# Two additions of a graph attention layer issued on GpSimd, with a new pace for the side work

## The chip, the cores and the metric

The kernel runs on one core of a Trainium2 chip. The core has a matrix engine (TensorE, "PE" in the profile, its weight loads "PEld"), a vector engine (VectorE, "DVE"), a scalar engine (ScalarE, "ACT") and a general engine (GpSimd, "POOL"), each with its own instruction queue that runs in order. A fifth queue ("SP") issues most DMAs. Engines meet at semaphores. The metric is the time of one execution on the device, in microseconds, as the median of several runs.

## The reference

Four graph layers run one after another on a graph of N = 2708 nodes with 128 features. Every layer normalises x, applies a ReLU, computes something with the adjacency matrix and adds the result to x. The adjacency is sparse: an entry is not zero with a probability of 0.0015, or on the diagonal, so that a node has some five neighbours, itself among them; the values lie between 0.05 and 1, and the kernel's lists hold up to 16 of them. The layer that matters here is the second:

```python
q = (x @ Wq.T).reshape(d, n, h)      # d = 128 channels, n = 2708 nodes, h = 8
k = (x @ Wk.T).reshape(d, n, h)
v = (x @ Wv.T).reshape(d, n, h)
a = jnp.einsum('dnh,dmh->dnm', q, k) * scale
a = a + spatial_encoding + edge_encoding     # adj + adj
a = jax.nn.softmax(a, axis=2)
out = jnp.einsum('dnm,dmh->dnh', a, v)
out = out.reshape(n, h * d)
return out @ Wo.T
```

So there are 128 attentions ("channels" below) over all 2708 nodes, with a head of 8 values.

## The kernel before

The kernel never forms the 2708 x 2708 attention matrices. The exponential of the small product q.k is written as a polynomial, so that the sum over all m becomes a product of features of q with moments of features of k and v. Where the adjacency is not zero, a correction is added: the weight exp(q.k) times (exp(2 adj) - 1), times v and times one. A column of ones beside the eight columns of v gives the softmax's denominator, so that each result has VW = 9 values, of which the ninth is the share of the denominator.

The polynomial runs in a loop over the 128 channels (variable d), and for each channel over six chunks of up to four node tiles (variable c). There are NT = 22 tiles of 128 nodes, the last with 20. All engines' instructions of this loop are written out in a fixed order by hand (a manual schedule). In each chunk:

- `evaluate` (line 1078 and after) multiplies the transposed features of q (fT) by the weighted moments (mw) on TensorE into g_ps, of which there are two buffers. VectorE multiplies by features bq (z, line 1094) and sums (o_raw, line 1100).
- `queries` makes the next channel's features fq on VectorE (helper line 1007); `turn` transposes them on TensorE, and ScalarE copies them to fT (line 1076).
- `keys` (in the first chunk) makes the features bk and fk of the keys two channels ahead on GpSimd, twelve instructions of helper line 1010; `with_values` makes y in two halves (in the third and the last chunk), one instruction of line 1010 each, into two buffers in turn.
- `moments` multiplies y and fk of the next channel on TensorE into m_ps (line 1048), and `weighted` (line 1058, once a channel) turns the sum into mw on VectorE.
- After every fourth channel (a group; there are 32) `sums` adds the constant term on GpSimd (line 693) and stores the group in o_g.

Beside the loop run two streams of side work, written as generators. The first is the variable `first`. After every chunk `owed` grows by PACE, and while it is at least one, `first` is advanced to its next `yield`; such an advance is called a step here. The stream has, in this order: a search for the neighbours in ten tiles of adjacency (`search`), taking turns with the copies of q, k and v by node (`by_node`); a sort of the nodes by number of neighbours (`in_order`); and the neighbours' terms (`from_neighbours`). The sort lets tile t have only ROOM[t] neighbours, 121 over all tiles. For each of these 121 (index b) `from_neighbours` does:

- `load(b + 1)`: an indirect DMA on GpSimd's queue gathers the k and v of one neighbour for each node (c_kv, line 825, three buffers); at a tile's first neighbour also q (c_q, line 817).
- `logits(b)`: the product q k (c_z, line 840) and its sum over the head (c_c, line 844), both on VectorE, one step each.
- `store()`: where a tile is finished, an indirect DMA on GpSimd's queue writes c_acc to more_n (line 887).
- `values(b - 1)`: v times the weight on VectorE (line 870), the weight itself into the ninth column by ScalarE (line 869), and then the addition to the tile's sum c_acc (line 878). A tile's first neighbour writes c_acc itself, and nothing is added. c_acc has one buffer, so the next tile's first neighbour waits until the store has read it.
- `weigh(b)`: the exponential and the factor from the adjacency on ScalarE.

When `first` is done, the second stream starts, at most three advances a chunk (`step`). It takes entries of the list `beside`, at most two at a time. `normalise(g)` loads a group's sums (ro from o_g, co from more_n, on SP), adds them (line 930), takes the reciprocal of the ninth column (line 932), multiplies (line 933) and stores to o_c. `project_out(t)` loads o_c for a tile, multiplies by Wo on TensorE and adds to x (line 508). An entry may start when its group is below d // 4 - 1. What is left at the end of the loop over channels is done after it.

Layers three and four follow; the change touches nothing in them.

Of the kernel before, what the change touches and what calls it, by code (L numbers as in the profile page):

```python
# [11 lines left out]
ALU = mybir.AluOpType  # L12
# [31 lines left out]
def _cuts(n, w):  # L44

    return [(s, min(w, n - s)) for s in range(0, n, w)]
# [3 lines left out]
def gnn4_kernel(  # L50
# [22 lines left out]
    nc = tc.nc  # L73
# [156 lines left out]
    with ExitStack() as ph:  # L230
# [42 lines left out]
        with tc.manual_schedule():  # L273
# [8 lines left out]
            for t0, tw in _cuts(NT, 4):  # L282
# [3 lines left out]
                for t in range(t0, t0 + tw):  # L286
                    sz = rows[t][1]
# [109 lines left out]
    def to_heads(eng, dst, src, d, t0, nt, n=P):  # L397
        for p0, p1, c, r in runs(d, t0, n):
            eng.dma_start(dst[c : c + p1 - p0, r : r + nt], src[p0:p1])
# [116 lines left out]
    with ExitStack() as ph:  # L516
# [285 lines left out]
        def from_neighbours():  # L802

            nc.scalar.activation(cw, s_val, AF.Exp, scale=2.0)
            yield
            yield
            nc.vector.tensor_scalar_add(cw, cw, -1.0)
            todo = [(t, s0, w) for t in range(NT) for s0, w in _cuts(ROOM[t], S)]
            qs, kvs, cs, accs = {}, {}, {}, {}
            done = []  # L810

            def load(b):
                t, s0, w = todo[b]
                r0, sz = rows[t]
                if s0 == 0:
                    qs[t] = tm.tile([P, C, HEAD], FP, name="c_q", tag="c_q")
                    nc.gpsimd.indirect_dma_start(
                        out=qs[t][:sz].rearrange("p c k -> p (c k)"),
                        out_offset=None,
                        in_=q_n.rearrange("n c k -> n (c k)"),  # L820
                        in_offset=bass.IndirectOffsetOnAxis(ap=s_row[:sz, t], axis=0),
                    )
                kvs[b] = big.tile([P, S, C, 2, HEAD], FP, name="c_kv", tag="big")
                for e in range(w):
                    nc.gpsimd.indirect_dma_start(  # L825
                        out=kvs[b][:sz, e].rearrange("p c e k -> p (c e k)"),
                        out_offset=None,
                        in_=kv_n.rearrange("n c k -> n (c k)"),
                        in_offset=bass.IndirectOffsetOnAxis(
                            ap=s_nbr[:sz, t, s0 + e : s0 + e + 1], axis=0  # L830
                        ),
                    )

            def logits(b):
                t, s0, w = todo[b]
                sz = rows[t][1]
                cs[b] = sm.tile([P, S, C], FP, name="c_c")
                for e in range(w):
                    z = tm.tile([P, C, HEAD], FP, name="c_z", tag="tmp")
                    nc.vector.tensor_tensor(  # L840
                        z[:sz], kvs[b][:sz, e, :, 0], qs[t][:sz], ALU.mult
                    )
                    yield
                    nc.vector.reduce_sum(cs[b][:sz, e], z[:sz], axis=AX.X)
                    yield

            def weigh(b):

                t, s0, w = todo[b]
                sz = rows[t][1]  # L850
                c = cs[b]
                nc.scalar.activation(c[:sz, :w], c[:sz, :w], AF.Exp)
                for e in range(w):
                    nc.scalar.activation(
                        c[:sz, e], c[:sz, e], AF.Copy, scale=cw[:sz, t, s0 + e : s0 + e + 1]
                    )

            def values(b):
                t, s0, w = todo[b]
                sz = rows[t][1]  # L860
                c, kv = cs.pop(b), kvs.pop(b)
                if s0 == 0:
                    accs[t] = lp.tile([P, C, VW], FP, name="c_acc", tag="n_kv")
                acc = accs[t]
                for e in range(w):
                    z = acc
                    if s0 + e:
                        z = tm.tile([P, C, VW], FP, name="c_v", tag="tmp")
                    nc.scalar.copy(z[:sz, :, HEAD], c[:sz, e])
                    nc.vector.tensor_tensor(  # L870
                        z[:sz, :, :HEAD],
                        kv[:sz, e, :, 1],
                        c[:sz, e, :, None].to_broadcast([sz, C, HEAD]),
                        ALU.mult,
                    )
                    yield
                    if s0 + e:
                        nc.vector.tensor_tensor(acc[:sz], acc[:sz], z[:sz], ALU.add)  # L878
                        yield
                if s0 + w == ROOM[t]:  # L880
                    done.append(t)

            def store():
                while done:
                    t = done.pop()
                    sz = rows[t][1]
                    nc.gpsimd.indirect_dma_start(
                        out=more_n.rearrange("n c k -> n (c k)"),
                        out_offset=bass.IndirectOffsetOnAxis(ap=s_row[:sz, t], axis=0),
                        in_=accs.pop(t)[:sz].rearrange("p c k -> p (c k)"),  # L890
                        in_offset=None,
                    )

            load(0)
            if REM:
                none = tm.tile([P, C * VW], FP, name="none", tag="tmp")
                nc.gpsimd.memset(none, 0.0)
                nc.sync.dma_start(
                    more_n[N:].rearrange("n c k -> n (c k)"), none[: NT * P - N]
                )  # L900
            yield
            for b in range(len(todo) + 1):
                if b + 1 < len(todo):
                    load(b + 1)
                    yield
                if b < len(todo):
                    yield from logits(b)
                store()
                if b:
                    yield from values(b - 1)  # L910
                if b < len(todo):
                    weigh(b)
            store()
            yield
            yield

        def normalise(g):

            ro = tm.tile([P, NT, GRP, VW], FP, name="r_raw", tag="tmp")
            co = tm.tile([P, NT, GRP, VW], FP, name="r_more", tag="c_q")  # L920
            nc.sync.dma_start(ro.rearrange("p t i k -> p (t i k)"), o_g[g])
            nc.sync.dma_start(
                co.rearrange("p t i k -> p t (i k)"),
                more_n[:, g * GRP : (g + 1) * GRP].rearrange("(t p) i k -> p t (i k)", p=P),
            )
            for _ in range(AHEAD):
                yield "loaded"
            rs = sm.tile([P, NT, GRP], FP, name="r_rs")
            on = lp.tile([P, GRP, NT, HEAD], FP, name="r_on")
            nc.vector.tensor_tensor(ro, ro, co, ALU.add)  # L930
            yield
            nc.vector.reciprocal(rs, ro[:, :, :, HEAD])
            nc.vector.tensor_tensor(
                on.rearrange("p i t k -> p t i k"),
                ro[:, :, :, :HEAD],
                rs[:, :, :, None].to_broadcast([P, NT, GRP, HEAD]),
                ALU.mult,
            )
            for t0, nt, sz in ((0, NF, P), (NF, 1, REM)):
                for i in range(GRP if sz else 0):  # L940
                    to_heads(nc.sync, o_c, on[:sz, i, t0 : t0 + nt], g * GRP + i, t0, nt, sz)
            yield
# [20 lines left out]
        for t, (r0, sz) in enumerate(rows):  # L963
            need = min((((r0 + sz) * P - 1) // N) // GRP, NG - 1)
            while done <= need:
                beside.append((normalise(done), done, True))
                done += 1
                while late and late[0][1] <= done - 3:
                    beside.append(late.pop(0))
            late.append((project_out(tm, ps_t, woT, t), need, False))  # L970
# [24 lines left out]

        mid = NT // 2
        parts = [(0, mid), (mid, NT)]
        PACE = 1.30
        TM = max(b - a for a, b in parts)
        W = weights()  # L1000
        bks = [lp.tile([P, NT, B_W], FP, name=f"bk{i}") for i in range(2)]
# [104 lines left out]
        with tc.manual_schedule():  # L1106
# [19 lines left out]
            for d in range(D):  # L1126
                asked = queries(d + 1) if d + 1 < D else iter(())
                for c in range(NCH):
# [20 lines left out]
                    n += 1  # L1149
                    owed += PACE  # L1150
                    while owed >= 1 and first is not None:
# [228 lines left out]
    with ExitStack() as ph:  # L1380
# [9 lines left out]
        with tc.tile_pool(name="l3w", bufs=1) as wk_pool, tc.tile_pool(  # L1390
# [21 lines left out]
            z = tp.tile([1, 2 * C], FP, name="tab_z")  # L1412
# [29 lines left out]
        with tc.tile_pool(name="l3_more", bufs=2) as mp, tc.tile_pool(  # L1442
# [28 lines left out]
            with tc.For_i(0, rounds):  # L1471
                for t, (r0, sz) in enumerate(rows):
# [35 lines left out]
                    z = gated(mp, bn[:, t], sz, idx, val, 8)  # L1508
# [34 lines left out]
        for t, (_, sz) in enumerate(rows):  # L1543
# [6 lines left out]
            z = gated(gp, own[:, :C], sz, s_nbr[:, t], s_val[:, t, :k], k)  # L1550
# [51 lines left out]
```

## Time and profile before

| what | us |
|---|---|
| median of 3 runs | 4518.02 (4509.77 to 4524.34) |
| the profiled execution | 4486.52 |
| its span | 4484.7 |
| VectorE busy in the span | 3669.4 |
| GpSimd busy in the span | 2544.8 |
| line 878's additions, 99 of them, mean 2.507 us | 248.2 |
| line 930's additions, 32 of them, mean 1.377 us | 44.1 |

The profile is of one execution. "Busy" counts the time in which an engine has an instruction in work, which may include time in which the instruction itself stands still. A group of instructions is written as line, engine, operation, output<-inputs, partitions x elements, count, then the busy time and the mean duration in ns; what follows the second bar is the idle time of that engine right before these instructions and what ended it. In the row of slices each digit is the busy share, in tenths, of one fortieth of the span (112 us). A line of the order of time gives the start, the duration, the engine, the line and what was done; instructions of the same kind that follow each other are drawn together with their count. A line of waits gives who waited for whom, the total in us, the number of waits and the longest.

### The profile page before, as it was taken

Reading aid. Unit: us, or ns where it says so; the run is one execution under the profiler, and the core shown is the slowest. Engines: PE = TensorE matmul, PEld = TensorE weight load, DVE = VectorE, ACT = ScalarE, POOL = GpSimd, SP = SyncE. Lnnn points to the kernel's source line nnn. Section 1 sums busy time; section 2 is a strip of 40 time slices with the busy share of each in tenths; the row PEclk is TensorE's granted clock in tenths of the full one; section 3 lists DMA queues with packets and bytes.
Section 4 is the critical chain, followed back from the end, with each engine's and each line's share of the span. In section 5 each row is a group of like instructions: output and inputs, shape, how many; then the busy total and the mean of one; then the engine's idle time right before and its main releaser. Section 6 shows DMA issues by size and latency. Waiting matters only on the chain. (4 is left out here: it accounts for less than half of the span.)

```text
span 4484.7 us, 49573 instructions
## 1 busy us (share of the span) xinstructions
PE 3225.3 (72%) x17298; PEld 2876.7 (64%) x17298; DVE 3669.4 (82%) x4983; ACT 1100.2 (25%) x2497; POOL 2544.8 (57%) x2253
## 2 busy tenths in 40 slices
PE   7985778889966677677777676667676687839634
PEld 5952777788856666667666676667666677824323
DVE  5988889998868999999999998999899888831323
ACT  4255233334412222222222222222122111101201
POOL 0001766678858666677676676767576555300076
PEclk9987888999988888888888888888888788959555
DMA  4647334357702222222222222222222344447132
GB/s 186 227 154 294 86 101 110 87 126 171 164 9 84 79 75 76 89 81 83 87 76 88 77 92 78 85 86 94 86 88 88 76 97 95 107 108 262 51 100 79
DMA packets 402005, 480.24 MB, mean 107 GB/s; under 512 B 290672, under 2 KB 322098, under 8 KB 376916
## 3 DMA queue, kind: packets, MB, share of 16 engines
q1 hardware_dynamic: 370140, 308.03, 23.8%
q0 software_dynamic: 31600, 168.86, 11.2%
q8 instruction: 144, 2.36, 0.2%
q14 instruction: 121, 0.99, 0.1%
HBM read 363.13 MB, written 113.67 MB: 106 GB/s over the span
## 5 line engine op out<-in xcount | busy, mean ns | idle before, releaser
L1086 PE MATMUL g_ps<-mw,fT 128*128 128x189 f32 x5632 | 1213.3, 362 | 734.6 <-DVE mw L1058 501.9
L1086 PEld LDWEIGHTS g_ps<-mw,fT 128*128 128x128 f32 x5632 | 1032.8, 213 | 812.8 <-issue 642.2
L1010 POOL TENSOR_TENSOR y<-bk,raw 128x2079 f32<-128x2079 f32 x256 | 982.9, 3840 | 685.7 <-PE m_ps L1048 658.4
L1048 PE MATMUL m_ps<-y,fk 128*128 128x189 f32 (+1 forms) x5632 | 1108.1, 342 | 29.0 <-POOL y L1010 29.0
L1048 PEld LDWEIGHTS m_ps<-y,fk 128*128 128x128 f32 (+1 forms) x5632 | 969.2, 204 | 58.1 <-POOL y L1010 29.5
L1076 ACT COPY fT<-f_ps 128x512 f32<-128x512 f32 (+1 forms) x768 | 422.9, 551 | 1955.2 <-PE f_ps L1074 1954.3
L1094 DVE TENSOR_TENSOR z<-g_ps,bq 128x756 f32<-128x756 f32 (+1 forms) x768 | 669.1, 871 | 177.7 <-PE g_ps L1086 173.9
L1100 DVE TENSOR_REDUCE o_raw<-z 128x36 f32<-128x756 f32 (+1 forms) x768 | 672.5, 876 | 26.3
L1010 POOL TENSOR_TENSOR fk<-bk,raw 128x528 f32<-128x528 f32 (+1 forms) x512 | 526.5, 1058 | 0.0
L1074 PE MATMUL f_ps<-ident,fq 128*128 128x128 f32 x2816 | 490.8, 299 | 46.2 <-DVE fq L1007 44.6
L1074 PEld LDWEIGHTS f_ps<-ident,fq 128*128 128x128 f32 x2816 | 399.2, 157 | 83.9 <-issue 45.8
L1010 POOL TENSOR_TENSOR fk<-raw,bk 128x352 f32<-128x352 f32 (+1 forms) x512 | 337.3, 688 | 0.0
L840 DVE TENSOR_TENSOR c_z<-c_kv,c_q 128x1024 f32<-128x1024 f32 (+1 forms) x121 | 308.1, 2546 | 5.3 <-DMA c_kv<-kv_n,srt 5.3
L1007 DVE TENSOR_TENSOR fq<-bq,q_ps 128x528 f32<-128x528 f32 (+1 forms) x512 | 288.1, 605 | 0.0
L825 POOL DMA_INDIRECT c_kv<-kv_n,srt x121 | 139.1, 1150 | 244.3 <-DVE c_v L870 142.4
L1010 POOL TENSOR_TENSOR bk<-raw 128x88 f32<-128x88 f32 (+1 forms) x512 | 238.3, 496 | 34.6 <-DMA raw<-qkv_c 34.1
L878 DVE TENSOR_TENSOR c_acc<-c_acc,c_v 128x1152 f32<-128x1152 f32 (+1 forms) x99 | 248.2, 2507 | 2.5
L465 POOL MEMSET qkv<- 128x512 f32 x6 | 6.3, 1076 | 373.7 <-PE l_o L350 254.3
L870 DVE TENSOR_TENSOR c_v<-c_kv,c_c 128x1024 f32<-128x1024 f32 (+1 forms) x99 | 205.9, 2080 | 0.0
L1420 POOL DMA_INDIRECT g<-gate_d,srt x121 | 122.0, 1008 | 107.9 <-issue 105.1
L505 PE MATMUL l_o<-woT,o_cr 128*128 128x128 f32 (+1 forms) x352 | 94.8, 425 | 107.6 <-DMA o_cr<-o_c 68.6
L1007 DVE TENSOR_TENSOR fq<-q_ps,bq 128x352 f32<-128x352 f32 (+1 forms) x512 | 171.7, 378 | 0.0
(284 smaller groups left out, 3490.2 us busy)
## 6 DMA issues: line engine op xcount, KB each, us to landing
a_nat<-in_adj_dram SPq DMA_DIRECT2D x32, 1354.0 KB
qkv_c<-qkv SPq DMA_DIRECT2D x5, 6400.0 KB
a<-in_adj_dram SPq DMA_DIRECT2D x21, 1354.0 KB
kv_n<-n_kv SPq DMA_DIRECT2D x32, 672.0 KB
an<-in_adj_dram SPq DMA_DIRECT2D x15, 1354.0 KB
o_g<-o_raw SPq DMA_DIRECT2D x32, 396.0 KB
r_raw<-o_g SPq DMA_DIRECT2D x32, 396.0 KB
r_more<-more_n SPq DMA_DIRECT2D x32, 396.0 KB
```

What stands on the lines that cost most here:

```text
L825: nc.gpsimd.indirect_dma_start(out=kvs[b][:sz, e].rearrange("p c e k -> p (c e k)"), out_offset=None, in_=kv_n.rearrange("n c k -> n (c k) ...
L840: nc.vector.tensor_tensor(z[:sz], kvs[b][:sz, e, :, 0], qs[t][:sz], ALU.mult)
L870: nc.vector.tensor_tensor(z[:sz, :, :HEAD], kv[:sz, e, :, 1], c[:sz, e, :, None].to_broadcast([sz, C, HEAD]), ALU.mult,)
L878: nc.vector.tensor_tensor(acc[:sz], acc[:sz], z[:sz], ALU.add)
L1007: nc.vector.tensor_tensor(o, x, y, ALU.mult)
L1010: nc.gpsimd.tensor_tensor(o, x, y, ALU.mult)
L1048: nc.tensor.matmul(pms[d][:, : B_ALL * VW], fks[d][:sz, t], ys[d, h][:sz, m].rearrange("p k b -> p (k b)"), start=t == 0, stop=t == NT - 1,)
L1074: nc.tensor.transpose(pt[:, m], fqs[d][:, t0 + m], ident)
L1076: nc.scalar.copy(fts[d, c][:, :n], pt[:, :n])
L1086: nc.tensor.matmul(pg[:, m, : B_ALL * VW], ft[:, m], mws[d].rearrange("p k b -> p (k b)"), start=True, stop=True,)
L1094: nc.vector.tensor_tensor(z[:, :n], pg[:, :n, : B_ALL * VW].rearrange("p t (k b) -> p t k b", k=VW), bqs[d % 2][:, t0 : t0 + n, None, :B_A ...
L1100: nc.vector.reduce_sum(ros[g][:, t0 : t0 + n, i], z[:, :n], axis=AX.X,)
```

## The change

Line 878's addition is issued on GpSimd instead of VectorE. A tile's sum c_acc is still first written by VectorE and ScalarE, and then added to by GpSimd. The `yield` that stood behind the addition now stands ahead of it: two steps lie between the product c_v and its addition, and the addition falls into the step that also issues `weigh(b)` and `load(b + 2)`. The second `yield` is outside the condition, so that a tile's first neighbour takes a step more than before. Line 930's addition in `normalise` goes to GpSimd as well, and the reciprocal on VectorE follows it as before. PACE goes from 1.30 to 1.45 steps a chunk.

```diff
@@ -874,9 +874,9 @@
                         ALU.mult,
                     )
                     yield
+                    yield
                     if s0 + e:
-                        nc.vector.tensor_tensor(acc[:sz], acc[:sz], z[:sz], ALU.add)
-                        yield
+                        nc.gpsimd.tensor_tensor(acc[:sz], acc[:sz], z[:sz], ALU.add)
                 if s0 + w == ROOM[t]:
                     done.append(t)
 
@@ -927,7 +927,7 @@
                 yield "loaded"
             rs = sm.tile([P, NT, GRP], FP, name="r_rs")
             on = lp.tile([P, GRP, NT, HEAD], FP, name="r_on")
-            nc.vector.tensor_tensor(ro, ro, co, ALU.add)
+            nc.gpsimd.tensor_tensor(ro, ro, co, ALU.add)
             yield
             nc.vector.reciprocal(rs, ro[:, :, :, HEAD])
             nc.vector.tensor_tensor(
@@ -995,7 +995,7 @@
 
         mid = NT // 2
         parts = [(0, mid), (mid, NT)]
-        PACE = 1.30
+        PACE = 1.45
         TM = max(b - a for a, b in parts)
```

## The prediction

> **What bounds the kernel now.** I began with the page's first two parts: how busy each engine is, and when.
>
> ```profile
> PE 3225.3 (72%) x17298; PEld 2876.7 (64%) x17298; DVE 3669.4 (82%) x4983; ACT 1100.2 (25%) x2497; POOL 2544.8 (57%) x2253
> DVE  5988889998868999999999998999899888831323
> POOL 0001766678858666677676676767576555300076
> ```
>
> VectorE stands at 9 from slice 13 to 30, with GpSimd at 6 or 7. Next, the sums by stretch, cut where the work beside the loop over channels changes: by-node copies, sorting, the neighbours' terms, normalising, and what is left after the loop.
>
> ```profile
> 945.00:1226.00 281.00, 263.03 (x1657) 248.35 (x1658) 240.21 (x406) 117.10 (x228) 229.85 (x214) 0.99 0.73 165
> 1226.00:1372.00 146.00, 91.43 (x505) 85.79 (x505) 92.55 (x147) 24.71 (x56) 100.05 (x117) 0.81 0.10 25
> 1372.00:3528.00 2156.00, 1520.50 (x8281) 1424.84 (x8279) 2047.64 (x2444) 484.14 (x1222) 1487.42 (x1223) 0.84 0.25 83
> 3528.00:3932.00 404.00, 322.68 (x1741) 305.46 (x1741) 327.72 (x491) 64.46 (x147) 202.95 (x173) 0.88 0.45 103
> 3932.00:4018.00 86.00, 27.48 (x112) 25.24 (x112) 26.18 (x48) 0.00 (x0) 2.40 (x1) 0.54 0.52 123
> ```
>
> The columns are length, then PE, PEld, DVE, ACT and POOL busy, the granted clock, DMA share and GB/s. In the third row VectorE works 2048 of 2156 us (95%), TensorE 71%, GpSimd 69%. The same view of line 1058, which runs once a channel, counts 16, 5, 74 and 14 channels in the first four rows: 17.6 us a channel where TensorE sets the pace (263 of 281 us), 29.1 us beside the neighbours, 28.9 us beside the normalising. So the neighbours' stretch is bound by VectorE. Its groups there, by shape:
>
> ```profile
> L840 DVE TENSOR_TENSOR c_z<-c_kv,c_q 128x1024 f32<-128x1024 f32 x119 | 299.7, 2518 | 5.3 <-DMA c_kv<-kv_n,srt 5.3
> L878 DVE TENSOR_TENSOR c_acc<-c_acc,c_v 128x1152 f32<-128x1152 f32 x98 | 243.9, 2488 | 2.5
> L870 DVE TENSOR_TENSOR c_v<-c_kv,c_c 128x1024 f32<-128x1024 f32 x98 | 204.7, 2089 | 0.0
> L1010 POOL TENSOR_TENSOR y<-bk,raw 128x2079 f32<-128x2079 f32 x150 | 582.1, 3881 | 345.7 <-PE m_ps L1048 335.5 <-DMA raw<-qkv_c 9.0
> ```
>
> And the lines' own views (shortest/median/longest, ns):
>
> ```profile
> L878 DVE TENSOR_TENSOR c_acc<-c_acc,c_v x99: 1337/1754/8283, 1415.0 to 3524.0; 128x1152 f32<-128x1152 f32 x98, 20x1152 f32<-20x1152 f32 x1
> L693 POOL TENSOR_TENSOR o_raw<-o_raw,v_sum x32: 1854/1874/2912, 564.9 to 3931.9; 128x792 f32<-128x792 f32 x32
> ```
>
> The addition takes 1.34 us at its shortest and 2.49 in the mean. The order of time shows where the rest comes from:
>
> ```profile
> 2551.16 1.39 POOL L1010 TENSOR_TENSOR bk<-raw 128x176 f32<-128x176 f32 x4
> 2551.66 8.28 DVE L878 TENSOR_TENSOR c_acc<-c_acc,c_v 128x1152 f32<-128x1152 f32 x1
> 2552.52 2.37 POOL L1010 TENSOR_TENSOR fk<-raw,bk 128x352 f32<-128x352 f32 x4
> 2554.86 3.86 POOL L1010 TENSOR_TENSOR fk<-bk,raw 128x528 f32<-128x528 f32 x4
> ```
>
> A VectorE instruction with both inputs in SBUF stood until GpSimd's twelve had run, then did its 1.3 us. z (line 1094), with an input in PSUM, shows no such thing (725 to 970 ns). Last, the waits of that stretch:
>
> ```profile
> POOL c_kv L825 <- DVE c_v L870: 142.4, 50, 9.3
> DVE c_acc L870 <- DMA more_n<-c_acc,srt: 49.0, 11, 9.2
> DVE z L1094 <- PE g_ps L1086: 33.1, 48, 1.6
> ```
>
> VectorE waited for TensorE before only 48 of 448 z, 33 us in all: time taken from VectorE here is time saved, until TensorE's pace is met.
>
> **The change, part by part.** Line 878's additions leave VectorE: page row 99 x 2.507 = **-248 us**, of which 99 x 1.34 = 133 are work and 115 waiting for GpSimd.
>
> On GpSimd they cost 99 x 2.70 = 267 us: line 693 takes 1.87 us for 792 elements, 2.34 ns each, times 1152. Line 1010's y would give 3.78 us / 2079 x 1152 = 2.10; I take 2.70, from a plain two-input addition nearest in size. GpSimd has 2156 - 1487 = 669 us without work in this stretch, so the work fits if it falls there. Each addition is issued two steps after its product c_v, just ahead of the next c_kv load, which already waited for that product 50 times. Behind it in GpSimd's queue stand this load, the store of more_n and the keys' and y's products. The load is wanted only when VectorE comes to that neighbour's logits, some four steps later (a step is 29.1/7.8 = 3.7 us), and VectorE waited for one 5 us in all: 0.
>
> What is late next is what remains on VectorE with two SBUF inputs: c_z, c_v and the first c_acc products. Their waits today: 308.1 - 121 x 1.21, plus 205.9 - 99 x 1.21, plus 22 x (1.56 - 1.21) = 162 + 86 + 8 = about 255 us. GpSimd's products fill 1248 + 46 of 2156 us, 60%. With 267 more in a stretch some 200 shorter, and five channels fewer (5 x 17.4), it is 75%. In proportion the waits grow by a quarter, +64. If each lasts until GpSimd is idle, as in the lines above, they also grow as idle time shrinks from 40 to 25%: 255 x (1.25 x 1.6 - 1) = +255. About half the loads (50 of 121) found GpSimd waiting for c_v; there the addition runs at once, under z and reductions that it doesn't disturb. I take **+90**, nearer the low end for that.
>
> The Trainium skill (SBUF — State Buffer, section Who interferes with whom) has a VectorE instruction with two SBUF inputs and a reading GpSimd instruction exclude each other for a whole instruction, the loser blocked. That agrees as to who blocks whom, but one instruction would bound a wait by y's 3.8 us, and the trace shows 8.28; by it I would stay at +64, and the sum would be 26 us lower.
>
> The store of a finished tile now follows its last addition in GpSimd's queue, and the next tile's first product waits for the landing (49 us on VectorE now, one buffer): between 0 and 22 x 2.7 = 59, **+30**. With less of its own work VectorE meets TensorE more often: the 33 us at z double, **+35** (0 to 70).
>
> The pace, 1.30 to 1.45 steps a chunk, six chunks a channel. I count the steps from the code: 80 + 192 for search and by-node, 30 for sorting, 587 for neighbours; 889 / 7.8 = 114.0 channels, and the normalising does begin at the 114th. Now 22 steps more (one for each tile's first neighbour): 911 / 8.7 = 104.7. So 9.3 channels move behind the side work. Where VectorE is the bound each leaves about 16.6 us (its share of z, reductions, fq, mw: 5.2 + 5.2 + 4.7 + 0.3 + 1.0 by the rows, less small overlaps, and TensorE's 17.6 in the early rows): -155. At the end a channel alone costs 17.6 x 0.99 / 0.88 = 19.8 us. The fourth row is then 14 x 19.8 = 277 plus 127 for 26 groups normalised, 4.9 each; with 23.3 channels and 30 groups 461 + 147 = 608, +204. After the loop only two groups and the last projections stay (the queue lets group k start when k is below the channel's group less one). In the order of time group 30 is loaded at 3981 and all is over at 4018: 37 us, and some 3 for the loop's own end make 40 of the 86, -46. Together **+3** (-40 to +40).
>
> Normalising: line 930's addition goes to GpSimd, 1.87 for 0.98 us, and the reciprocal behind it on VectorE, with z behind that, now waits for GpSimd's queue. I set each of the 32 additions of the old run, in order of time, against what had been issued to GpSimd ahead of it: all of it was finished in 24 cases, and the other eight lags are 0.2 to 3.2 us, 8.6 together (0.27 a group). So 1.87 - 0.98 + 0.27 and some 0.1 for the hand-over, 1.26 x 32 = **+40**. The bounds are 0 where TensorE's own stalls hide it and 32 x 5 = 160 where it stands behind y or the keys. The landing that VectorE waited for (27 us) is now waited for on GpSimd.
>
> Sum: -248 + 90 + 30 + 35 + 3 + 40 = **-50 us**. The profiled execution took 4486.5 us, 0.7% under the median of 4518.0, so about 4436 for it, and **4468** by the median.
>
> **The rivals.** (1) Slower: GpSimd's additions displace VectorE's other two-input products. At the upper bound of +255 the sum is -248 + 255 + 30 + 35 + 3 + 40 = +115; it decides from waits of +140 (c_z and c_v near 3.0 us mean), where the sum is 0; with +200 it is +60, 4578. For it: the 8.28 us line, and GpSimd with work for 1487 / 74.3 = 20.0 us a channel now and 24.0 then. Against: the loads that found GpSimd waiting. The Trainium skill (Perfetto Trace Analysis, section Optimizing Scalar/DVE Operations) warns that moving work between these two might not help, since they share a read port. (2) Slower: the reciprocal waits for keys or y in most groups, +160 for +40: +70, 4588; against it is the lag above. (3) No change: waits at +140 or a pace that costs 40 cancel the gain, 4518.
>
> **How the numbers follow.** My forecast, faster with 4468 (its own range 4390 to 4504), gets 0.46; rival 1 0.28, rival 2 0.14, no change 0.12. Within 0.3% (14 us) is about what three runs that spread by 14.6 us can't tell from no change. Faster 0.46, same 0.12, slower 0.42. The low end of the range takes the waits at +40, the store and z at 0 and normalising at 10: -248 + 40 + 3 + 10 = -195, 4323, cut to 4365 as all must meet; the high end is rival 1 at its bound, +115 = 4633, cut to 4610.
>
> **What would show it.** Right: the neighbours' stretch near 1980 us (2156 - 248 + 155 - 86 for its 5.3 channels fewer) and 70 channels; c_z near 2.9 and c_v near 2.4 us mean; GpSimd's addition at 2.7; normalising from channel 105; some 40 us after the loop; the reciprocal's wait near 1.2 us. Wrong: c_z above 3.2 us, the wait for more_n well over 80 us, m_ps waiting for y on TensorE, or reciprocals waiting over 4 us each.

## The result, and the profile after

The changed kernel takes 4462.79 us in the median of four runs (4448.62 to 4488.88), against 4521.18 for the kernel before in the same measurement (4509.77 to 4527.50). The ratio is 0.9873, with an interval from 0.9844 to 0.9903: faster by some 1.3%. Measured again beside another series it was 0.9904 (0.9873 to 0.9935), 4458.43 us. The profiled execution took 4452.14 us, its span 4450.3, so 34 us less than the profiled one of before. The addition is line 879 now; the other lines have kept their numbers.

First the page of the changed kernel: the engines' busy time and two rows of slices.

```profile
PE 3230.9 (73%) x17298; PEld 2879.4 (65%) x17298; DVE 3549.0 (80%) x4852; ACT 1101.9 (25%) x2497; POOL 2789.4 (63%) x2384
...
DVE  5988899987849989999988999999977777840322
...
POOL 0001766677767887887878777678876666700266
```

99 + 32 additions have left VectorE, which held 292 us before, yet VectorE is busy only 120 us less (3669 to 3549). GpSimd has gained 245 (2545 to 2789) and stands at 7 and 8 where it stood at 6 and 7. The view by stretch, cut as before (by-node copies, sorting, neighbours' terms, normalising, after the loop; columns are length, then PE, PEld, DVE, ACT and POOL busy, clock, DMA share, GB/s):

```profile
946.00:1165.00 219.00, 199.46 (x1234) 187.50 (x1233) 174.60 (x296) 90.24 (x176) 171.54 (x158) 0.98 0.76 177
1165.00:1308.00 143.00, 92.93 (x511) 86.58 (x510) 89.88 (x147) 26.98 (x60) 100.37 (x117) 0.81 0.15 34
1308.00:3330.00 2022.00, 1429.92 (x7709) 1339.91 (x7708) 1890.27 (x2206) 458.78 (x1160) 1600.04 (x1249) 0.84 0.26 88
3330.00:3922.00 592.00, 494.00 (x2801) 465.85 (x2799) 449.04 (x732) 110.25 (x255) 395.10 (x331) 0.91 0.38 86
3922.00:3965.00 43.00, 15.36 (x65) 13.49 (x65) 8.15 (x24) 0.00 (x0) 5.56 (x3) 0.56 0.41 102
```

The third row is 134 us shorter, the fourth 188 longer, the last 43 shorter. VectorE still works 93% of the third row. The stages of all runs that follow are compared in one table ("changed again" is the second profile of the changed kernel); it is worked out from each trace's order of time, by the first and last instruction of each stage, and the number after the stroke counts channels by their z. "Rest" is layers three and four, which no kernel here changes; its spread of 25 us shows what stage times of single executions can't tell.

| kernel | search, by-node | sort | neighbours | normalise | after the loop | rest |
|---|---|---|---|---|---|---|
| before | 761 / 35.0 | 144 / 4.3 | 2157 / 74.7 | 401 / 14.0 | 87 | 466 |
| changed | 707 / 31.5 | 131 / 3.8 | 2023 / 69.3 | 590 / 23.3 | 43 | 486 |
| changed again | 706 | 138 | 2029 | 591 | 43 | 466 |
| pace only | 703 / 31.5 | 131 / 3.8 | 1984 / 66.8 | 649 / 25.8 | 42 | 483 |
| normalise only | 764 | 142 | 2167 / 74.7 | 383 / 14.0 | 92 | 489 |
| additions only | 759 | 142 | 2193 / 77.3 | 307 / 11.3 | 141 | 479 |
| normalise back | 705 | 137 | 2027 | 601 | 42 | 485 |
| no addition | 705 | 132 | 1867 / 69.3 | 589 | 43 | 466 |
| memsets instead | 710 | 131 | 1990 / 69.3 | 588 | 43 | 464 |
| half the additions | 707 | 137 | 2072 / 69.5 | 592 | 43 | 465 |
| pace 1.40 | 721 / 32.7 | 133 | 2073 / 72.5 | 560 / 19.0 | 43 | 468 |
| pace 1.60 | 685 / 28.5 | 131 / 3.0 | 1934 / 63.5 | 840 / 33.0 | 43 | 466 |
| one step earlier | 708 | 131 | 2016 / 69.3 | 592 | 43 | 466 |
| two steps earlier | 705 | 136 | 1988 / 69.3 | 591 | 43 | 466 |

The groups by shape in the changed kernel's neighbours' stretch (1308 to 3330 us), which answer to those of before:

```profile
L1010 POOL TENSOR_TENSOR y<-bk,raw 128x2079 f32<-128x2079 f32 x139 | 532.1, 3829 | 159.5 <-PE m_ps L1048 131.3 <-ACT c_c L854 11.5 <-DVE c_c L844 6.5
...
L840 DVE TENSOR_TENSOR c_z<-c_kv,c_q 128x1024 f32<-128x1024 f32 x119 | 413.5, 3474 | 10.6 <-DMA c_kv<-kv_n,srt 10.6
...
L879 POOL TENSOR_TENSOR c_acc<-c_acc,c_v 128x1152 f32<-128x1152 f32 x98 | 259.4, 2647 | 164.4 <-DVE c_v L870 119.1 <-issue 32.4 <-ACT c_c L854 10.5
L870 DVE TENSOR_TENSOR c_v<-c_kv,c_c 128x1024 f32<-128x1024 f32 x98 | 240.0, 2449 | 1.3 <-POOL c_acc L879 1.3
```

The products c_z take 3.47 us in the mean where they took 2.52, c_v 2.45 where it took 2.09. With the few other shapes and each tile's first product, c_z, c_v and c_acc are 712 us together, before 548: 164 us of the 248 have come back in them. The idle time of GpSimd ahead of y has gone from 346 us to 160: GpSimd runs late, and y finds the moments that had to read its buffer done. The order of time shows the worst place:

```profile
2590.44 2.62 POOL L879 TENSOR_TENSOR c_acc<-c_acc,c_v 128x1152 f32<-128x1152 f32 x1 [9.15 <-DVE c_v L870]
...
2593.74 14.60 DVE L840 TENSOR_TENSOR c_z<-c_kv,c_q 128x1024 f32<-128x1024 f32 x1
...
2594.19 3.79 POOL L1010 TENSOR_TENSOR y<-bk,raw 128x2079 f32<-128x2079 f32 x1
...
2597.92 1.88 POOL L693 TENSOR_TENSOR o_raw<-o_raw,v_sum 128x792 f32<-128x792 f32 x1
...
2599.74 1.37 POOL L1010 TENSOR_TENSOR bk<-raw 128x176 f32<-128x176 f32 x4
...
2601.08 2.36 POOL L1010 TENSOR_TENSOR fk<-raw,bk 128x352 f32<-128x352 f32 x4
...
2603.41 3.84 POOL L1010 TENSOR_TENSOR fk<-bk,raw 128x528 f32<-128x528 f32 x4
```

GpSimd waits 9.15 us for its addition's c_v; what has queued up behind then runs without a gap, y, the constant term and twelve instructions of the keys, 13 us, and a c_z of 1.2 us stands through all of it, although its record begins 0.45 us ahead of y's. Last, the waits of that stretch:

```profile
POOL y L1010 <- PE m_ps L1048: 131.3, 44, 9.7
POOL c_acc L879 <- DVE c_v L870: 119.1, 49, 9.2
DVE c_acc L870 <- DMA more_n<-c_acc,srt: 57.1, 12, 12.2
DVE z L1094 <- PE g_ps L1086: 44.1, 47, 1.8
```

The wait for the store has grown by 8 us only, the wait for TensorE by 11. In the second profile of the changed kernel the three products take 696 us, the wait for the store is 76.3 and that for TensorE 49.3, so that a sum of one profile is good to some 20 us.

### The profile page after: what moved, and what is told of

Its sections match the earlier page's. It is cut to its first block, busy times and chain, and to the rows that moved or that the text cites. A ratio compares the mean times of both kernels' runs of the same rounds, so it can differ in the third digit from the quotient of the medians.

```text
span 4450.3 us, 49671 instructions
## 1 busy us (share of the span) xinstructions
PE 3230.9 (73%) x17298; PEld 2879.4 (65%) x17298; DVE 3549.0 (80%) x4852; ACT 1101.9 (25%) x2497; POOL 2789.4 (63%) x2384
## 5 line engine op out<-in xcount | busy, mean ns | idle before, releaser
L1086 PE MATMUL g_ps<-mw,fT 128*128 128x189 f32 x5632 | 1227.8, 366 | 699.1 <-DVE mw L1058 397.8
L1010 POOL TENSOR_TENSOR fk<-bk,raw 128x528 f32<-128x528 f32 (+1 forms) x512 | 508.2, 1021 | 0.0
L1074 PEld LDWEIGHTS f_ps<-ident,fq 128*128 128x128 f32 x2816 | 400.5, 157 | 75.7 <-issue 31.5
L840 DVE TENSOR_TENSOR c_z<-c_kv,c_q 128x1024 f32<-128x1024 f32 (+1 forms) x121 | 419.5, 3467 | 10.6 <-DMA c_kv<-kv_n,srt 10.6
L879 POOL TENSOR_TENSOR c_acc<-c_acc,c_v 128x1152 f32<-128x1152 f32 (+1 forms) x99 | 262.1, 2647 | 165.6 <-DVE c_v L870 119.1
L1010 POOL TENSOR_TENSOR fk<-raw,bk 128x352 f32<-128x352 f32 (+1 forms) x512 | 317.7, 649 | 0.0
L870 DVE TENSOR_TENSOR c_v<-c_kv,c_c 128x1024 f32<-128x1024 f32 (+1 forms) x99 | 244.5, 2470 | 1.3 <-POOL c_acc L879 1.3
L1010 POOL TENSOR_TENSOR bk<-raw 128x88 f32<-128x88 f32 (+1 forms) x512 | 216.7, 454 | 33.4 <-DMA raw<-qkv_c 32.9
```

Source lines behind the costliest of these rows:

```text
L840: nc.vector.tensor_tensor(z[:sz], kvs[b][:sz, e, :, 0], qs[t][:sz], ALU.mult)
L870: nc.vector.tensor_tensor(z[:sz, :, :HEAD], kv[:sz, e, :, 1], c[:sz, e, :, None].to_broadcast([sz, C, HEAD]), ALU.mult,)
L879: nc.gpsimd.tensor_tensor(acc[:sz], acc[:sz], z[:sz], ALU.add)
L1010: nc.gpsimd.tensor_tensor(o, x, y, ALU.mult)
L1074: nc.tensor.transpose(pt[:, m], fqs[d][:, t0 + m], ident)
L1086: nc.tensor.matmul(pg[:, m, : B_ALL * VW], ft[:, m], mws[d].rearrange("p k b -> p (k b)"), start=True, stop=True,)
```

## The experiments

The theory at this point: the additions' 248 us are gained, and the gain is eaten by the waits of VectorE's other two-input products, since GpSimd's queue is fuller. Rivals were that an addition on GpSimd excludes these products itself, for its own 2.65 us; that the pace, not the additions, brings the gain; and that the normalising gives something back.

### The three parts alone

Pace only, in the kernel before:

```diff
-        PACE = 1.30
+        PACE = 1.45
```

> The kernel before with PACE 1.45 alone. My theory (the gain is VectorE's relief beside the neighbours, and the pace by itself moves work without gaining): 4521 +3 us, between 4490 and 4550; normalising begins near channel 102, the stretch beside the neighbours is 5 channels shorter but each channel there dearer, near 30.3 us, and what is left after the loop falls from 86 to about 40 us. Rival (the whole gain is the tail that the pace empties, and the moved additions give nothing): 4521 - 50, near 4470.

Measured: 4498.24 us, ratio 0.9949 (0.9924 to 0.9974). Its neighbours' stretch, normalising and the time after the loop, in the view by stretch:

```profile
1302.00:3287.00 1985.00, 1384.71 (x7428) 1294.51 (x7428) 1897.66 (x2239) 447.44 (x1134) 1368.03 (x1122) 0.82 0.26 89
3287.00:3936.00 649.00, 546.02 (x3083) 518.72 (x3081) 527.16 (x829) 122.20 (x281) 382.12 (x330) 0.90 0.34 81
3936.00:3978.00 42.00, 15.76 (x65) 13.94 (x65) 10.58 (x24) 0.00 (x0) 1.85 (x1) 0.55 0.42 105
```

Beside the kernel before, 11.9 channels have left the first three stages, which became 244 us shorter (20.5 us each); the normalising took in 11.8 and became 248 longer (21.0 each). These two are even, and the 45 us saved after the loop are what the profile shows as the gain; by the ratio the gain is 0.5%, 23 us. That is within the range of my theory, though not at its +3, and half of what the rival put.

Normalising only, in the kernel before:

```diff
-            nc.vector.tensor_tensor(ro, ro, co, ALU.add)
+            nc.gpsimd.tensor_tensor(ro, ro, co, ALU.add)
```

> The kernel before with line 930's addition alone on GpSimd. My theory: +40 us (4561), the reciprocal's waits near 1.2 us each. Rival (hidden under TensorE's own stalls there, as the shorter normalising stretch of the changed kernel hints): 4521 within 14 us.

Measured: 4509.91 us, 0.9970 (0.9951 to 0.9989), 14 us faster; the theory's +40 failed. Its waits from 3540 us on, and the line of the kernel before that answers to the first:

```profile
POOL r_raw L930 <- DMA r_more<-more_n: 98.8, 10, 16.4
...
DVE r_rs L932 <- POOL r_raw L930: 65.7, 21, 10.0
```

```profile
DVE r_raw L930 <- DMA r_more<-more_n: 26.8, 6, 7.5
```

The reciprocals wait 66 us for GpSimd, yet the kernel is no slower. Before, the addition stood in VectorE's queue for its landing, 26.8 us, with z and the sums behind it; now GpSimd stands for it, 98.8 us, and VectorE goes on. The normalising stretch is 18 us shorter.

Additions only (the changed kernel with the old pace and line 930 on VectorE):

```diff
-            nc.gpsimd.tensor_tensor(ro, ro, co, ALU.add)
+            nc.vector.tensor_tensor(ro, ro, co, ALU.add)
...
-        PACE = 1.45
+        PACE = 1.30
```

> The kernel before with line 878's addition on GpSimd and its two yields, at the old pace 1.30 and with line 930 on VectorE. My theory: -248 +155 (the waits of c_z and c_v as the changed kernel shows them, somewhat fewer at this pace) and about 20 for store and z, but 22 more steps at 1.30 move 2.8 channels less behind: near 4455, with 100 us or more left after the loop. Rival (the pace makes the gain): 4521 within 20 us.

Measured: 4488.57 us, 0.9906 (0.9874 to 0.9939), 43 us faster by the ratio, between the theory and its rival. The additions are the largest of the three, and they pay for the 22 added steps, which the pace of 1.30 makes visible. The third line is the time after the loop:

```profile
1371.00:3564.00 2193.00, 1572.61 (x8606) 1479.14 (x8604) 2014.78 (x2420) 497.54 (x1253) 1730.01 (x1365) 0.84 0.24 82
3564.00:3870.00 306.00, 247.60 (x1346) 235.11 (x1346) 248.91 (x385) 50.71 (x117) 153.09 (x129) 0.89 0.46 105
3870.00:4011.00 141.00, 43.53 (x177) 40.57 (x177) 41.66 (x79) 0.00 (x0) 1.87 (x1) 0.53 0.56 131
```

The neighbours' terms now lie beside 77.3 channels, and 141 us of normalising and projecting are left over for the end, where nothing covers them; 87 before.

The changed kernel with line 930 back on VectorE:

```diff
-            nc.gpsimd.tensor_tensor(ro, ro, co, ALU.add)
+            nc.vector.tensor_tensor(ro, ro, co, ALU.add)
```

> The changed kernel with line 930's addition back on VectorE. My theory: 40 us faster than the changed kernel, near 4425. Rival (hidden): 4463 within 14 us.

Measured: 4461.56 us, 0.9859 (0.9813 to 0.9905). The changed kernel itself has 0.9873 and 0.9904; the intervals overlap. At the new pace no difference shows between the two places of line 930; the theory's 40 us failed again. The three parts alone add up to -1.8%, more than the whole gives (-1.3 and -1.0%): they don't add up simply, since the same channels are moved and the same end is shortened.

### What the additions cost where they are

No addition at all: the sums keep only each tile's first neighbour.

```diff
                     yield
                     yield
-                    if s0 + e:
-                        nc.gpsimd.tensor_tensor(acc[:sz], acc[:sz], z[:sz], ALU.add)
```

> The changed kernel without line 878's additions: the sums keep only each tile's first neighbour, all else is as before. What remains of the price of the additions on GpSimd goes. Theory A (they cost by displacing VectorE's c_z, c_v and c_acc products, whose waits grew from 255 to some 400 us): c_z falls back to 2.4 us and c_v to 2.0 in the mean, and the time falls by 130 to 190 us, near 4300. Theory B (the gain was eaten by TensorE's pace and the stores, not by these waits): the waits stay and the time falls by less than 50 us, above 4410.

Measured: 4294.82 us, 0.9539 (0.9504 to 0.9574), as theory A put it (c_v falls only to 2.28 us). Its neighbours' stretch, and its c_z in the page:

```profile
1304.00:3171.00 1867.00, 1405.99 (x7699) 1322.46 (x7698) 1741.70 (x2202) 457.56 (x1159) 1335.76 (x1151) 0.86 0.29 95
```

```profile
L840 DVE TENSOR_TENSOR c_z<-c_kv,c_q 128x1024 f32<-128x1024 f32 (+1 forms) x121 | 296.9, 2454 | 8.5 <-DMA c_kv<-kv_n,srt 8.5
```

So the changed kernel pays 156 us for 99 additions on GpSimd (1867 to 2023), 3.3 to 3.7% by the ratios, and its VectorE is 149 us longer at work there (1742 to 1890; 1876 in the second profile). From the kernel with the new pace alone, where the additions are on VectorE and hold it 240 us, to none at all it is 4.1%, 185 us (line 930 and the 22 added steps differ as well). Part of the rest is waiting that passes on: of the 240 us 133 are work (99 x 1.34) and 107 waiting, and without the additions c_z, c_v and each tile's first c_acc take 567 us together where they took 523, so that 44 of the 107 have come back.

Memsets in their place, three for each addition, of together about the same length. They write the used c_v tile and read nothing; the sums again keep only the first neighbour.

```diff
-                        nc.gpsimd.tensor_tensor(acc[:sz], acc[:sz], z[:sz], ALU.add)
+                        nc.gpsimd.memset(z[:sz], 0.0)
+                        nc.gpsimd.memset(z[:sz], 0.0)
+                        nc.gpsimd.memset(z[:sz, : C // 2], 0.0)
```

> The changed kernel with each of line 878's additions replaced by three memsets of the product's tile on GpSimd, about 2.7 us together, which write SBUF and read nothing; the sums keep only each tile's first neighbour. GpSimd's queue is as full as with the additions. Theory A1 (the price is the exclusion of two SBUF-reading instructions): within 30 us of the kernel without the addition, c_z near 2.4 us. Theory A2 (the price is the delay of GpSimd's queue, so that its products fall later onto VectorE's): within 30 us of the changed kernel, 4463, c_z near 3.4 us.

Measured: 4407.86 us, 0.9799 (0.9761 to 0.9836), between the two theories. The neighbours' stretch, then c_z in the page, then a place in the order of time:

```profile
1310.00:3301.00 1991.00, 1433.54 (x7717) 1348.05 (x7715) 1835.22 (x2209) 459.50 (x1161) 1593.06 (x1450) 0.84 0.27 89
```

```profile
L840 DVE TENSOR_TENSOR c_z<-c_kv,c_q 128x1024 f32<-128x1024 f32 (+1 forms) x121 | 336.4, 2780 | 7.8 <-DMA c_kv<-kv_n,srt 7.7
```

```profile
2390.71 1.06 POOL L880 MEMSET c_v<- 128x1152 f32 x1
...
2390.77 1.22 DVE L840 TENSOR_TENSOR c_z<-c_kv,c_q 128x1024 f32<-128x1024 f32 x1
...
2391.82 0.58 POOL L881 MEMSET c_v<- 128x576 f32 x1
```

A c_z that starts under a memset takes 1.22 us, as short as they get (1.20): the memset doesn't stop it. All the same the stretch is 123 us longer than without anything (1867 to 1990), of the additions' 156. So most of the price is not the addition's own exclusion.

I set each of VectorE's two-input instructions of the neighbours' terms, beyond its shortest time, against what GpSimd ran meanwhile. The additions that stay on VectorE count too (in the first two kernels all, in one half). The sums are in us; "over 4" counts instructions that waited more than 4 us.

| kernel | waiting | under y | under the keys | under the additions | over 4 |
|---|---|---|---|---|---|
| before | 369 | 235 | 133 | - | 15 |
| pace only | 336 | 189 | 147 | - | 17 |
| no addition | 273 | 153 | 112 | - | 11 |
| memsets instead | 361 | 236 | 114 | 0 | 25 |
| changed | 418 | 225 | 156 | 30 | 27 |
| changed again | 403 | 219 | 151 | 25 | 28 |
| half the additions | 420 | 241 | 166 | 9 | 33 |
| one step earlier | 372 | 210 | 135 | 18 | 24 |
| two steps earlier | 307 | 165 | 114 | 21 | 18 |

From no addition to the changed kernel the waiting grows by 145 us (130 in the second profile), of which 30 (25) lie under the additions and 116 (105) under y and the keys, whose own work is the same. With the memsets it grows by 88, 85 of it under y and the keys. What is put into GpSimd's queue costs VectorE mainly through the instructions behind it. Longer runs are part of this. Take as a run what follows each other on GpSimd with less than 0.1 us between (y, keys, constant terms, additions): runs of over 8 us number 51 without the addition (642 us), 63 with the memsets (760 us) and 60 in the changed kernel (782 us; 55 and 735 us in the second profile). The runs alone don't set the price, since the kernel before has 66 of them (864 us) and less waiting.

Every second addition on GpSimd:

```diff
-                        nc.gpsimd.tensor_tensor(acc[:sz], acc[:sz], z[:sz], ALU.add)
+                        eng = nc.gpsimd if b % 2 else nc.vector
+                        eng.tensor_tensor(acc[:sz], acc[:sz], z[:sz], ALU.add)
```

> The changed kernel with every other of line 878's additions on VectorE and the rest on GpSimd. If the waits grow in proportion to GpSimd's additions: between the kernel with the pace alone (4498) and the changed kernel (4463), near 4480. If they grow faster than in proportion as idle time goes: less than both, 4440 to 4455, with c_z below 2.8 us.

Measured: 4479.94 us, 0.9944 (0.9925 to 0.9964): no better than the pace alone (0.9949). The additions in its groups:

```profile
L880 DVE TENSOR_TENSOR c_acc<-c_acc,c_v 128x1152 f32<-128x1152 f32 (+1 forms) x47 | 167.1, 3555 | 0.0
...
L880 POOL TENSOR_TENSOR c_acc<-c_acc,c_v 128x1152 f32<-128x1152 f32 x52 | 138.7, 2667 | 123.0 <-DVE c_v L870 74.7 <-issue 26.9 <-ACT c_c L854 18.3
```

With the pace alone all 99 are on VectorE:

```profile
L878 DVE TENSOR_TENSOR c_acc<-c_acc,c_v 128x1152 f32<-128x1152 f32 (+1 forms) x99 | 240.3, 2428 | 3.0
```

The 47 that stay on VectorE take 3.56 us each, with the pace alone 2.43. So half of the additions take 73 us off VectorE (240 to 167) and not 120, and the waiting is 420 us as with all of them. The price isn't in proportion to the number moved, and the other theory (faster than both) failed as well; why half costs it all is not settled. One difference that these runs don't separate: in this kernel a sum passes from GpSimd to VectorE and back.

### The pace

The changed kernel with other paces:

```diff
-        PACE = 1.45
+        PACE = 1.60
```

> The changed kernel at pace 1.60. Side work ends at channel 95, and the channels that move behind it cost 18 us alone at the end against what they save among the neighbours. Theory (a channel fewer beside the neighbours saves about 20 us, as the pace alone showed, near the 18 to 19 us that it costs behind): 4463 within 20 us, nothing more in the tail (43 us stay). Rival (the pace goes on to gain in proportion): 4463 - 25.

Measured: 4564.31 us, 1.0132 (1.0086 to 1.0178), some 100 us above the changed kernel, where both theory and rival put it level or below. The normalising stretch, and a wait in it:

```profile
3219.00:4060.00 841.00, 683.20 (x3899) 646.85 (x3899) 628.00 (x989) 159.49 (x370) 548.44 (x474) 0.89 0.28 66
```

```profile
DVE r_rs L932 <- POOL r_raw L930: 76.2, 18, 8.5
```

Beside the changed kernel 9.6 channels more have left the first three stages, which became 111 us shorter: 11.6 us each. The normalising took in 9.7 for 250 us: 25.8 each. In the order of time its last 18 channels follow a beat of four, mostly 27.2, then 19 to 22, 17.9 and 17.9 us, 20.9 on average: two of four are as short as a channel gets here, and no side work is left to fill them. Of the 32 reciprocals 18 wait, 4.2 us each, 2.4 over all.

```diff
-        PACE = 1.45
+        PACE = 1.40
```

> The changed kernel at pace 1.40. Side work ends at channel 108.5 instead of 104.7. A channel moved from behind the side work to beside it costs about 15 to 20 us there (1.45 against 1.60 gave 15, 1.30 against 1.45 gave 22) and saves 18 to 21 us behind, and the tail stays at 43 us as 19 channels are still enough for 30 groups: theory, 0 to 20 us faster than the changed kernel, ratio to the kernel before 0.983 to 0.988. Rival (1.45 is past no optimum): ratio above 0.990.

Measured: 4488.62 us, 0.9975 (0.9950 to 0.9999); the theory failed. In its normalising stretch (560 us) there are 19 channels, 29.5 us each, and only the last two come down to 17.5 and 17.9:

```profile
3395.00:3955.00 560.00, 433.47 (x2346) 410.90 (x2346) 392.44 (x618) 89.27 (x207) 330.81 (x274) 0.86 0.39 88
```

The time after the loop is 43 us, as at 1.45. A pace on either side is worse than 1.45. For 1.60 the two sums show where the time goes; why a channel less beside the neighbours saves so little there (11.6 us, and 20.5 from 1.30 to 1.45) they don't show. For 1.40 nothing here shows the cause: the profiled execution, 4468 us, was the shortest of twelve that reached 4522, so that its stages aren't those of the median. That stays open.

### Where the addition is issued

The addition one step earlier, and two:

```diff
                     yield
-                    yield
                     if s0 + e:
                         nc.gpsimd.tensor_tensor(acc[:sz], acc[:sz], z[:sz], ALU.add)
+                    yield
```

> The changed kernel with the second yield behind the addition again, so that the addition is issued one step after its product instead of two, and a step ahead of the next load. If the price is only how full GpSimd's queue is: the changed kernel within 15 us, c_z near 3.4 us. If the place matters (GpSimd then waits for the product more often, and y and the keys behind it come later): slower by 20 us or more, with more than 119 us of waiting for c_v.

Measured: 4431.47 us, 0.9851 (0.9825 to 0.9877), beside 0.9904 (0.9873 to 0.9935) for the changed kernel, which ran in the same series as it is; the two intervals only just overlap. Neither alternative came: GpSimd waits longer for c_v (126.6 us), and the kernel is not slower. The changed kernel's second run:

> The changed kernel once more beside these two: ratio 0.987 within 0.004, and the stages of its first profile within 15 us each.

Then right behind the product:

```diff
-                    yield
-                    yield
                     if s0 + e:
                         nc.gpsimd.tensor_tensor(acc[:sz], acc[:sz], z[:sz], ALU.add)
+                    yield
+                    yield
```

> The changed kernel with the addition issued in the product's own step, and both yields behind it. If what one step earlier gained goes on (ratio 0.985 against 0.990 for the changed kernel on the same chip; the waits of the two-input products 372 us against 403): ratio near 0.981 and c_z below 3.0 us. If GpSimd now stands waiting for the product with y and the keys behind it: ratio above 0.990, over 127 us of waiting for c_v, and less waiting of y for TensorE than 94 us.

Measured: 4398.27 us, 0.9764 (0.9740 to 0.9787), the fastest of all the kernels that compute the whole, 102 us below the kernel before (4500.05 in its series). Its neighbours' stretch (cut 5 us early; in its own place, 1310 to 3297, the busy times are the same within 1 us), its c_z in the page, and three of its waits:

```profile
1305.00:3292.00 1987.00, 1427.35 (x7720) 1341.89 (x7719) 1780.16 (x2201) 457.65 (x1160) 1605.71 (x1254) 0.84 0.26 89
```

```profile
L840 DVE TENSOR_TENSOR c_z<-c_kv,c_q 128x1024 f32<-128x1024 f32 (+1 forms) x121 | 330.0, 2727 | 22.8 <-DMA c_kv<-kv_n,srt 22.8
```

```profile
POOL c_acc L877 <- DVE c_v L870: 132.6, 55, 7.0
DVE c_acc L870 <- DMA more_n<-c_acc,srt: 125.6, 19, 13.3
POOL y L1010 <- PE m_ps L1048: 53.0, 15, 9.8
```

GpSimd does the same work, and VectorE is busy 110 us less than in the changed kernel (1890 to 1780; 96 against its second profile). The waiting of the table above has gone from 418 or 403 to 372 and 307 us with the two places. In return VectorE waits 126 us for the store of more_n where it waited 57 (76), so that the stretch is only 35 us (41) shorter in the profile; a second buffer for c_acc would be the next thing to try, and was not tried. GpSimd's idle time as a whole is smaller than in the changed kernel (1987 - 1606 = 381 against 2022 - 1600 = 422), so it isn't the amount of idle time that frees VectorE. It has moved: 239 us ahead of the additions where there were 166, 53 ahead of y for m_ps where there were 131. One might think that these gaps fall just where VectorE has its two-input products to do, but in the order of time only 36 of the 242 products begin in a gap ahead of an addition, 26 in the changed kernel. Nor do fewer products meet GpSimd at work: 187 begin while it has an instruction, 180 in the changed kernel and 176 without the additions. What differs is how long such a product stands, 1.6, 2.3 and 1.5 us, and most of the gain is c_z's (272 us of waiting in the changed kernel, 183 here). So the products come at other moments of GpSimd's runs; why this place of issue brings them there is open.

## Why the prediction was right, and where its steps were not

The forecast, 4468 us, lies 5 us from what was measured. The direction and the main steps held (VectorE is the bound, it gains the additions, and part comes back in its other products), but the sum came this close by luck, because its errors cancelled. By stages it stands like this: search and sort were to give -69 (9.3 channels at 16.6, less the neighbours' 86) and gave -67; the neighbours' stretch was to give -179 and gave -134; normalising +244 (the channels' 204 and line 930's 40) and gave +189; the end -46 and gave -44. The sums are -50 and -56. (In the changed kernel's first profile layers three and four took 20 us more, which the change can't have caused; the second profile has them at 466 as before.) By its terms:

- **The additions leave VectorE, -248.** This holds as time that VectorE no longer spends on them. As a gain it is about 185 us (pace alone to no addition). The step counted 115 us of waiting as gained; part of such waiting passes on to the other two-input products (44 of 107 us above).
- **The waits that remain, +90.** Measured +164 (+148 in the second profile; +189 from the kernel with the pace alone, 523 to 712), between the bounds of 64 and 255, but the choice near the low end failed. Its reason was that half the additions would run as soon as c_v is there, under work that they don't disturb. They do (49 waits for c_v, 119 us, against 50 loads before), and only 30 us of waiting lie under the additions. The step priced the addition by what it disturbs itself, and the waiting grew under y and the keys, which stand behind it. The sign that was to prove the forecast wrong, c_z above 3.2 us, came (3.47), and so did rival 1's turning point of +140. Rival 1 still didn't happen, because that point was worked out with +108 for the four terms below.
- **The store, +30; VectorE meeting TensorE, +35.** Measured +8 (49.0 to 57.1) and +11 (33.1 to 44.1), in the second profile +27 and +16. Doubling the wait for TensorE was too much for any VectorE here: even without the additions z waits 48.8 us.
- **The pace, +3.** Measured alone it is -23 us (-0.5%). The end was right, 40 us for 43. The channels were counted right too (104.7 in the first three stages), but a channel that leaves the neighbours' stretch took 22 us with it in the run with the pace alone (173 us for 7.9) and not 16.6, so that the moved channels come out even instead of costing 49.
- **Normalising, +40.** Measured -14 at the old pace and nothing at the new one. The duration was right (60.3 us for 32, 1.88 each) and the reciprocal does wait (58.8 us, 1.84 each, for 1.26 put). What failed is that this wait was taken as lying on the path: GpSimd has taken over the wait for the landing, and rows of z and sums can go on. Rival 2, over 4 us for each reciprocal, appears in no run: at a pace of 1.60 the 18 that wait take 4.2 us, which is 2.4 for each of the 32.
- **GpSimd's room.** 2.65 us an addition, where the row of line 693 had given 2.70. The load of the next neighbour cost nothing, as put: VectorE waited 10.6 us for one, before 5.3.

The measured terms make -248 + 164 + 8 + 11 - 23 + 0 = -88 where the kernels differ by 58: they come from different pairs of kernels, and time taken off VectorE is not all time saved.

On the rule that the prediction weighed (the Trainium skill, SBUF — State Buffer, section Who interferes with whom): its half that a GpSimd instruction which only writes doesn't contend agrees with the memsets here, under which 16 products started and waited less than 0.1 us in all. The bound of one whole instruction, which the prediction took from it, doesn't hold in these traces: a product stood 8.28 us before and 14.60 us after, through fourteen of GpSimd's, and 27 products waited over 4 us, more than y's mean of 3.83, 13 of them longer than the longest y (4.84 us). That bound is not what decides between +64 and +164, though: with each single wait cut off at 4.84 us, the waits would still grow by 136 us (233 to 369). Most of the growth is in waits that fit within one instruction.

## What to carry to other kernels

Where two engines exclude each other, price an instruction that is moved from one to the other by the waits that it adds behind it in the other's queue, and not by its own length: here each addition of 2.65 us lengthened the stretch by some 1.6 us, and waiting under the additions themselves makes 0.3 of it. Try the place of issue before giving a move up or accepting it: the same change with the additions issued right behind their products, and not two steps later, gave 2.4% where it had given 1.0 to 1.3%. And when a sum of terms meets the measurement, check the terms one by one, since most of the six were off by 20 to 70 us here and their sum by 5.

## What was not expected of the hardware

A VectorE product with two inputs in SBUF can stand through a whole run of GpSimd instructions that have no gap between them: 14.60 us for fourteen, at a product of 1.2. And instructions that read nothing (memsets, 1.06 us each, under which such a product ran in 1.22 us) still made the stretch 123 us longer over 99 places, while VectorE waited 85 us more under the y and keys that queue up among them.
